# Expert-choice FFN: all block products of the hidden stage by inner products, gathers through the turned tokens' buffer, another order of sums in the output stages

## The chip, the cores and the metric

The kernel runs on one core of a Trainium2 chip. The metric is the device time of one execution in microseconds (us). The engines are named as in the profile: PE does matmuls, PEld loads their weights, DVE, ACT and POOL are the vector, scalar and GpSimd engines, and SP issues DMAs.

## The reference, cut to what matters

Eight sequences of 512 tokens of width D = 512 go through a modulated dense layer. A router gives each of E = 8 experts the k = 1024 tokens with the highest scores, each expert runs a two-layer network on its tokens, and the results are added back to the tokens' rows.

```python
y = ...                                  # modulated dense layer, (4096, 512)
scores = softmax(y @ Wr)                 # (4096, 8)
G, idx = top_k(scores.T, 1024)           # per expert
X_in = y[idx]                            # (8, 1024, 512)
h = gelu(einsum('ekd,edh->ekh', X_in, W1) + b1)      # hidden width 2048
X_e = einsum('ekh,ehd->ekd', h, W2) + b2
out = zeros.at[idx.reshape(-1)].add((G[..., None] * X_e).reshape(-1, 512))
return x + out.reshape(x.shape)
```

All of it is fp32.

## The kernel before

After a front (dense layer, router, choice of the tokens, some 165 us) the kernel works expert by expert (e = 0 to 7), each in two passes (p = 0, 1) over halves of the hidden width. A pass is a *hidden stage*, H = gelu(X W1 + b1), and an *output stage*, H W2, whose rows are scaled by the gain and added to DRAM by an indirect scatter. Both stages use the Strassen-Winograd scheme: a product of 2 x 2 blocks is made of seven block products and additions on DVE.

**Hidden stage.** There are seven outer products (numbered 1 to 7) of token sums with weight sums. Products 2 to 7 are themselves done by seven *inner products* of 128x256 outputs with K = 128 (`second_level`), in two halves a and b of the rows of the result. Product 1 is done *whole* (`one_product`): for each of four units two matmuls into a bank of 128x512 (`ps_a_h`), which ACT copies to `snap1` (L1215). The order of all steps on the engines follows a list written by hand, `ORDER`: "2b5" is inner product 5 of outer product 2, half b, "1.0" to "1.3" are the units of product 1, "h" stands for a leftover step of the output stage before. The first stage of all (e = p = 0) uses only the outer scheme (`hidden_unit`); the other fifteen follow ORDER.

An inner product's results are accumulated in PSUM banks. Tag a has two banks, tag b one, tag c two, and some of the a products lie in two banks of another pool. ACT evicts the a banks (L1129, L1153), DVE the b bank (L1138, inner product 2) and the c banks (L1149 after inner product 5, L1157 after inner product 4). When outer products are complete, DVE adds them (L1218, L1231, L1233, L1235) and ACT applies the gelu (L1219).

**Work between.** Behind certain steps of ORDER (the places of "1.0" to "1.3") other work is issued, ahead of the steps that follow it: at place 2 (behind "2b2 1.1") the four sums of W2's blocks on DVE (128x1024 each, L211 to L214), at place 0 of pass 1 the gathers of the next expert's tokens (`fetch`).

**Output stage.** Four units v, each of seven products of four matmuls 128x256 (`ps_a_o`, `ps_b_o`, `ps_c_o`), with four `left_sums` of H on DVE (128x512, L973 to L976), evictions by ACT and DVE (L1345 to L1391) and two scatters (L1378). `in_turns` interleaves the units. Between them lies other work: behind unit 2 the sums of the next pass's W1 (4 x 128x1024, then the second-level sums, 4 x 128x1024 for products 2, 7, 3, 4 in one tile `w1_l2` and 8 x 128x256 for products 5 and 6, L224 to L238), behind unit 0 of pass 1 `prepare(e+1)` (four transposes of the gathered tokens, L1018, four left sums of 128x1024, and their second-level sums, again 4 x 128x1024 and 8 x 128x256), behind unit 1 of pass 0 `indices(e+1)`.

**Tokens.** `gather` reads 128 rows at a time from DRAM by an indirect DMA on POOL's queue (L957) into tiles `row`, stores them to DRAM (`rows`, L961, SP's queue) and loads them turned into two tiles of tag `xg` (L963). The scatters of the output stage (L1378) are on POOL's queue too, and each adds to rows of one DRAM tensor.

Of the kernel before, what the change touches and what calls it, by code (L numbers as in the profile page):

```python
# [20 lines left out]
P = 128  # L21
# [4 lines left out]
def tile_modulated_expert_choice_ffn(  # L26
# [123 lines left out]
    for n in range(15):  # L150
# [18 lines left out]
    L2 = (2, 7, 3, 4)  # L169
# [3 lines left out]
        6a1 h 6a6 6a2 h 2a1 6a7 6a5 2a6 2a2 1.0 5a1 6a3 2a7 2a5 6a4 5a6 5a2 1.2 7a1  # L173
        2a3 5a7 5a5 2a4 7a6 7a2 4a1 5a3 7a7 7a5 5a4 4a6 4a2 3a1 7a3 4a7 4a5 7a4 3a6 3a2
        2b1 4a3 3a7 3a5 4a4 2b6 2b2 1.1 6b1 3a3 2b7 2b5 3a4 6b6 6b2 5b1 2b3 6b7 6b5 2b4
        5b6 5b2 1.3 7b1 6b3 5b7 5b5 6b4 7b6 7b2 3b1 5b3 7b7 7b5 5b4 3b6 3b2 4b1 7b3 3b7
        3b5 7b4 4b6 4b2 3b3 4b7 4b5 3b4 4b3 4b4
# [3 lines left out]
    def weight_blocks(kind, where, name):  # L181


        out = {}
        if kind == "w1":
            out["l2"] = wpool.tile([P, len(L2), 2, U * P], F32, tag="w1_l2", name=f"w1_l2_{name}")
        for (i, j), src in where.items():
            shape = [P, 2, U * P] if kind == "w1" else [P, U, QD]
            if kind == "w1" and (i, j) != (0, 0):
                t = out["l2"][:, L2.index({(1, 0): 2, (1, 1): 3, (0, 1): 7}[i, j]), :, :]  # L190
            else:
                t = wpool.tile(shape, F32, tag=f"{kind}_{i}{j}", name=f"{kind}_{i}{j}_{name}")
            if isinstance(src, list):
                for k in range(4):
                    nc.sync.dma_start(t[k * TB : (k + 1) * TB, :, :], src[k])
            else:
                nc.sync.dma_start(t, src)
            out[i, j] = t
        return out

    def weight_sum_steps(kind, blk, name):

        shape = [P, 2, U * P] if kind == "w1" else [P, U, QD]
        t1 = wpool.tile(shape, F32, tag=f"{kind}_t1", name=f"{kind}_t1_{name}")
        t2 = wpool.tile(shape, F32, tag=f"{kind}_t2", name=f"{kind}_t2_{name}")
        if kind == "w1":
            t4 = blk["l2"][:, L2.index(4), :, :]
        else:
            t4 = wpool.tile(shape, F32, tag=f"{kind}_t4", name=f"{kind}_t4_{name}")
# [6 lines left out]
    def weight_sums(kind, blk, name):  # L216
        for _ in weight_sum_steps(kind, blk, name):
            pass
        if kind == "w1":
# [11 lines left out]
            for which, base in ((5, blk["t1"]), (6, blk["t2"])):  # L231
                b = {(k, j): base[:, k, j * Q : (j + 1) * Q] for k in range(2) for j in range(2)}
                t = fx.tile([P, 3, Q], F32, tag=f"w1_sums{which}", name=f"w1_sums{which}_{name}")
                t1, t2, t4 = [t[:, n, :] for n in range(3)]
                nc.vector.tensor_add(t1, b[0, 0], b[0, 1])
                nc.vector.tensor_add(t2, t1, b[1, 1])
                nc.vector.tensor_add(t4, t2, b[1, 0])
                nc.vector.tensor_add(b[0, 1], b[0, 1], b[1, 1])  # L238
                blk["l2", which] = {**b, "t1": t1, "t2": t2, "t3": b[0, 1], "t4": t4}
# [636 lines left out]
    def indices(e):  # L876
# [4 lines left out]
        hot = rt2.tile([P, NT, KG], BF16, tag="hot", name=f"hot_{e}", bufs=1)  # L881
# [4 lines left out]
        val = rt2.tile([P, NT, 2, KG], BF16, tag="val", name=f"val_{e}", bufs=1)  # L886
# [57 lines left out]
    gathered = {}  # L944
# [3 lines left out]
    def gather(e, i):  # L948


        z = gp.tile([P, GH * YW], F32, tag="xg", name=f"xg_{e}_{i}")
        rows = dram.tile([HALF, YW], F32, name=f"rows_{e}_{i}")
        z = z[:, 0 : GH * D].rearrange("p (t c) -> p t c", c=P)
        for j in range(GH):
            g = i * GH + j
            to = gp.tile([P, YW], F32, tag="row", name=f"row_{e}_{g}")
            sent = nc.gpsimd.indirect_dma_start(  # L957
                out=to[:, :], out_offset=None, in_=y_dram[:, :],
                in_offset=bass.IndirectOffsetOnAxis(ap=idx[:, e, g : g + 1], axis=0),
            )  # L960
            nc.sync.dma_start(rows[j * P : (j + 1) * P, :], to)  # L961
        for q in range(4):
            nc.sync.dma_start(z[q * TB : (q + 1) * TB, :, :],  # L963
                              rows[:, q * P : (q + 1) * P].rearrange("(t a) c -> a t c", a=TB))
        with nc.allow_non_contiguous_dma(reason="512 values"):
            nc.sync.dma_start(gains[e][:, i * GH : (i + 1) * GH],
                              rows[:, D + e : D + e + 1].rearrange("(g p) o -> p (g o)", p=P))
        gathered[e, i] = z
        return sent

    def left_sums(a11, a12, a21, a22, s):
# [4 lines left out]
        nc.vector.scalar_tensor_tensor(s["s4"], s["s2"], -1.0, a12, op0=ALU.mult, op1=ALU.subtract)  # L976
# [3 lines left out]
    def token_tiles(e):  # L980
        l2 = fx.tile([P, len(L2), 2, HALF], F32, tag="x_l2", name=f"x_l2_{e}")
        base = {which: l2[:, m, :, :] for m, which in enumerate(L2)}
        xT = {(0, 1): base[2], (1, 1): base[4]}
        for k in range(2):
            xT[k, 0] = fx.tile([P, 2, HALF], F32, tag=f"xT{k}0", name=f"xT{k}0_{e}")
        s = {n: fx.tile([P, 2, HALF], F32, tag=f"x{n}", name=f"x{n}_{e}") for n in ("s1", "s2")}
        s["s3"], s["s4"] = base[7], base[3]
        gain = gains.pop(e)
        ngain = fx.tile([P, KG], F32, tag="ngain", name=f"ngain_{e}")
        tokens[e] = {**s, "11": xT[0, 0], "12": xT[0, 1], "22": xT[1, 1], "l2": l2}, gain, ngain  # L990
        return xT, s, gain, ngain

    def second_sums(e):
# [4 lines left out]
        more = fx.tile([P, 2, len(L2), Q], F32, tag="x_sums", name=f"x_sums_{e}")  # L998
        s2 = {"s1": a[1, 0], "s2": more[:, 0, :, :], "s3": more[:, 1, :, :],
              "s4": fx.tile([P, len(L2), Q], F32, tag="xT10", name=f"x_s4_{e}")}  # L1000
# [4 lines left out]
        for which, base in ((5, s["s1"]), (6, s["s2"])):  # L1005
            a = {(i, k): base[:, k, i * Q : (i + 1) * Q] for i in range(2) for k in range(2)}
            more = fx.tile([P, 3, Q], F32, tag=f"x_sums{which}", name=f"x_sums{which}_{e}")
            s2 = {"s1": a[1, 0], **{f"s{n + 2}": more[:, n, :] for n in range(3)}}
            left_sums(a[0, 0], a[0, 1], a[1, 0], a[1, 1], s2)
            s["l2", which] = {**s2, "11": a[0, 0], "12": a[0, 1], "22": a[1, 1]}  # L1010

    def prepare(e):
# [10 lines left out]
        second_sums(e)  # L1023

    def first_tokens(started):
# [4 lines left out]
        for j in range(GH):  # L1030
            for i in range(2):
                g = i * GH + j
                sent = nc.gpsimd.indirect_dma_start(
# [3 lines left out]
        with tc.issue_after(sent.ins):  # L1037
# [28 lines left out]
    def in_turns(units, between, keep=False):  # L1066
# [6 lines left out]
        for n in range(len(units)):  # L1073
# [12 lines left out]
            for work in between.get(n, ()):  # L1086
                with tc.issue_after(mark.ins):
                    work()
# [12 lines left out]
    def second_level(e, p, which, r, H, third):  # L1101
# [4 lines left out]
        if which in (5, 6):  # L1106
            lie = [sp.tile([P, HALF], F32, tag="snap4" if which == 5 else "snap2",
# [53 lines left out]
    def hidden_stage(e, p, H, between, held, then):  # L1161
# [3 lines left out]
        units = [one_product(e, p, u, H) for u in range(U)]  # L1165
        inner, left, mark = {}, {}, None
        place = [n for n, o in enumerate(ORDER) if "." in o and o[0] == "1"]
        place = {n: m for m, n in enumerate(place)}
        held = list(held)
        for n, o in enumerate(ORDER):  # L1170
            ready = []
# [4 lines left out]
            elif "." in o:  # L1176
                which, u = int(o[0]), int(o[2])
                units[u][which]()
                left[which, u] = True
                ready = [u]  # L1180
            else:
# [4 lines left out]
                todo = left.setdefault(("steps", which, r), set(range(1, 8)))  # L1186
                todo.discard(step)
                if not todo:
                    for u in (r, r + 2):
                        left[which, u] = True  # L1190
                        if which in (5, 6):
                            units[u][f"q{which}"](inner[which, r]["lie"][u // 2])
                    ready = [r, r + 2]
            for u in ready:
                units[u]["add"](left, u)
            if n in place:
                for work in between.get(place[n], ()):
                    with tc.issue_after(mark.ins):
                        work()

    def one_product(e, p, u, H):


        s, blk = tokens[e][0], w1_blocks[e, p]
        name = f"h{e}_{p}_{u}"
        bias = [b1_sb[:, e, p * HP + j * U + u : p * HP + j * U + u + 1] for j in range(2)]
        out = {(i, j): H[:, u, j, i * HALF : (i + 1) * HALF] for i in range(2) for j in range(2)}
        st, done = {}, set()

        def whole():  # L1210
            ps = bank("a", name, 2)
            product(ps, [blk[0, 0][:, k, u * P : (u + 1) * P] for k in range(2)],
                    [s["11"][:, k, :] for k in range(2)], True)
            st[1] = sp.tile([P, HALF], F32, tag="snap1", name=f"snap1_{name}", bufs=2)
            nc.scalar.copy(st[1], ps)  # L1215
# [5 lines left out]
        def add(there, u):  # L1221

            def can(name, *needs):
                if name in done or not all((n, u) in there or n in done for n in needs):
                    return False
                done.add(name)
# [268 lines left out]
```

## Time and profile before

| | us |
|---|---|
| median of 3 runs | 1692.82 (1692.28 to 1692.93) |
| the profiled execution, its own time | 1686.02 |
| its span in the profile | 1684.2 |
| hidden stage of expert 1, pass 1 | 465 to 506 |
| output stage after it | 506 to 558 |

The clock granted to PE is 0.996 of full speed in this execution. In a line of a timeline the columns are start, duration, engine, line of the kernel, operation, output and inputs, and in brackets how long the engine sat idle before it and what released it. Durations of neighbours overlap, so what one instruction costs in a row is read from the start to the next start. Inputs and outputs go by the program's names, with numbers left out: `ps_c_qc` is a c bank of a hidden stage, `ps_a_o` an a bank of an output stage, `w_t`, `w_sums`, `w_l` are sums and blocks of the weights, `hs_o` are left sums.

### The profile page before, as it was taken

How to read it: one execution, taken by the hardware profiler on the slowest of the kernel's cores; microseconds unless marked ns; L12 is line 12 of the kernel's file. 1: busy time of each engine (PE TensorE's matmuls, PEld its weight loads, DVE VectorE, ACT ScalarE, POOL GpSimd, SP SyncE). 2: the span in 40 equal slices, each digit the busy share in tenths (PEclk: the TensorE clock that was granted, in tenths of full speed). 3: DMA queues.
4: the chain of work that ended last, by engine and by line, in shares of the span. 5: the costliest groups of instructions: out<-in, count | busy, mean ns of one | idle time of the engine just before them, and what ended most of it. 6: DMA issues, size and time to landing. Idle time of an engine off the chain costs nothing.

```text
span 1684.2 us, 21423 instructions
## 1 busy us (share of the span) xinstructions
PE 1652.2 (98%) x7726; PEld 1335.6 (79%) x7726; DVE 1325.1 (79%) x2544; ACT 652.8 (39%) x1445; POOL 349.9 (21%) x238
## 2 busy tenths in 40 slices
PE   9997999999999999999999999999999999999997
PEld 5785567888878788888888788888888787888886
DVE  5885798978779686978789686978698786967681
ACT  3543323526152533425161524435261625344351
POOL 0111003220411213030412123030412132030202
PEclk9999999999999999999999999999999999999999
DMA  9724714742563337342653336342743247242403
GB/s 211 180 52 152 245 42 95 212 83 66 124 140 76 69 89 180 97 83 62 143 137 74 68 95 170 88 89 57 185 116 75 45 114 186 70 77 63 88 1 50
DMA packets 143273, 178.83 MB, mean 106 GB/s; under 512 B 16824, under 2 KB 92856, under 8 KB 143040
## 3 DMA queue, kind: packets, MB, share of 16 engines
q1 hardware_dynamic: 118240, 115.19, 24.2%
q0 software_dynamic: 24912, 62.27, 21.1%
q8 instruction: 60, 0.98, 0.3%
q14 instruction: 45, 0.37, 0.1%
q10 hardware_dynamic: 16, 0.02, 0.0%
HBM read 120.46 MB, written 65.37 MB: 110 GB/s over the span
## 4 chain that ended last, share of the span: by engine, by line
PE 71%; DVE 9%; DMA 1%; issue 1%; ACT 1%; POOLq 0%; POOL 0%; DVEq 0%
PE ps_a_o L1098 18%; PE ps_qa L1098 12%; PE ps_c_o L1098 10%; PE ps_c_qc L1098 9%; PE ps_a_qa L1098 6%; PE ps_a_h L1098 6%; PE ps_b_o L1098 5%; PE ps_b_qb L1098 5%; DMA out<-o_o,idx 1%; DVE x_l L1018 1%; DVE x_sums L975 1%; DVE x_sums L973 1%; DVE xs L974 1%; DVE hs_o L975 1%; DVE hs_o L973 1%
## 5 line engine op out<-in xcount | busy, mean ns | idle before, releaser
L1378 POOL DMA_INDIRECT out<-o_o,idx x128 | 257.2, 2009 | 1128.3 <-DVE o_o L1375 317.5
L1345 ACT ACTIVATE snap_o<-ps_a_o,gain 128x256 f32<-128x256 f32 x128 | 59.8, 472 | 332.2 <-PE ps_a_o L1098 315.0
L1129 ACT ACTIVATE q<-ps_qa 128x256 f32<-128x256 f32 x360 | 137.7, 383 | 127.7 <-PE ps_qa L1098 78.0
L1219 ACT ACTIVATE H<-H,b_sb 128x512 f32<-128x512 f32 x240 | 166.3, 718 | 37.3 <-DVE H L1218 31.9
L1098 PE MATMUL ps_a_o<-w,H 128*128 128x256 f32 x512 | 129.2, 383 | 3.4 <-ACT o_o L1386 3.4
L1098 PE MATMUL ps_b_o<-w,H 128*128 128x256 f32 x512 | 127.1, 379 | 0.0
L1098 PE MATMUL ps_a_o<-w_t,hs_o 128*128 128x256 f32 x512 | 123.8, 382 | 1.7 <-DVE hs_o L975 1.7
L1098 PE MATMUL ps_c_o<-w,hs_o 128*128 128x256 f32 x512 | 122.9, 382 | 0.0
L1098 PE MATMUL ps_c_o<-w_t,H 128*128 128x256 f32 x504 | 119.6, 380 | 2.8 <-DVE o_o L1370 2.8
L1098 PE MATMUL ps_a_o<-w,hs_o 128*128 128x256 f32 x512 | 121.8, 381 | 0.0
L1098 PE MATMUL ps_a_o<-w_t,H 128*128 128x256 f32 x512 | 121.3, 379 | 0.0
L1218 DVE TENSOR_TENSOR H<-H,q 128x512 f32<-128x512 f32 x180 | 118.3, 684 | 3.0 <-ACT H L1153 0.2
L1098 PE MATMUL ps_a_h<-xT,w 128*128 128x512 f32 x248 | 119.3, 593 | 0.0
L1098 PEld LDWEIGHTS ps_a_o<-w_t,hs_o 128*128 128x128 f32 x512 | 95.6, 190 | 20.4 <-DVE hs_o L975 4.1
L1098 PEld LDWEIGHTS ps_a_o<-w,H 128*128 128x128 f32 x512 | 95.5, 190 | 19.0 <-ACT o_o L1386 5.8
L1098 PEld LDWEIGHTS ps_c_o<-w,hs_o 128*128 128x128 f32 x512 | 95.9, 190 | 18.3 <-DVE hs_o L973 5.4
L1098 PEld LDWEIGHTS ps_c_o<-w_t,H 128*128 128x128 f32 x504 | 95.2, 190 | 16.9 <-DVE o_o L1370 4.0
L1098 PEld LDWEIGHTS ps_a_o<-w,hs_o 128*128 128x128 f32 x512 | 94.6, 190 | 16.8 <-ACT snap_o L1345 3.9
L1098 PEld LDWEIGHTS ps_b_o<-w,H 128*128 128x128 f32 x512 | 97.2, 190 | 13.5 <-DVE o_o L1356 0.3
L1098 PEld LDWEIGHTS ps_a_o<-w_t,H 128*128 128x128 f32 x512 | 96.3, 190 | 14.4 <-issue 0.5
L1345 ACT ACTIVATE snap_o<-ps_a_o,ngain 128x256 f32<-128x256 f32 x64 | 30.3, 473 | 175.0 <-PE ps_a_o L1098 175.0
L1129 ACT ACTIVATE q<-ps_a_qa 128x256 f32<-128x256 f32 x180 | 68.4, 380 | 59.0 <-PE ps_a_qa L1098 42.2
(357 smaller groups left out, 3338.9 us busy)
## 6 DMA issues: line engine op xcount, KB each, us to landing
w<-in_w SPq DMA_DIRECT2D x78, 512.0 KB, 5.0
w_l<-in_w SPq DMA_DIRECT2D x42, 512.0 KB, 5.0
rows<-row SPq DMA_DIRECT2D x56, 260.0 KB, 2.3
xg<-rows SPq DMA_DIRECT2D x56, 256.0 KB, 4.9
x<-in_x SPq DMA_DIRECT2D x28, 256.0 KB, 8.2
y_dram<-ytok SPq DMA_DIRECT2D x5, 1024.0 KB, 4.3
w_l<-in_w SPq DMA_DIRECT2D x24, 128.0 KB, 3.5
y_dram<-ytok POOLq DMA_DIRECT2D x12, 256.0 KB, 5.0
```

Source lines behind the costliest of these rows:

```text
L973: nc.vector.tensor_sub(s["s3"], a11, a21)
L974: nc.vector.tensor_sub(s["s1"], a22, a21)
L975: nc.vector.scalar_tensor_tensor(s["s2"], s["s3"], -1.0, a22, op0=ALU.mult, op1=ALU.subtract)
L1018: nc.vector.transpose(xT[i, k].rearrange("p j (t b) -> p t j b", b=TB), xg[:, :, 2 * k * TB : 2 * (k + 1) * TB].rearrange("p t (j a) -> p ...
L1098: nc.tensor.matmul(ps, lefts[k], rights[k], start=(start and k == 0), stop=(k == n - 1), skip_group_check=True)
L1129: nc.scalar.mul(t, st["a"], scale)
L1218: nc.vector.tensor_add(out[i, j], out[i, j], st[n])
L1219: nc.scalar.activation(out[i, j], out[i, j], AF.Gelu, bias=bias[j], scale=scale)
L1345: nc.scalar.mul(t, st["a"], scale)
L1378: nc.gpsimd.indirect_dma_start(out=last_rows[g] if e == E - 1 else out_rows, out_offset=bass.IndirectOffsetOnAxis(ap=idx[:, e, g : g + 1], ...
```

## The change

1. Outer product 1 is done by inner products too. The operands of all seven outer products lie in one tile (`w1_l2` and `x_l2`, seven slots), so that second-level sums become four instructions of 128x1792 each for the weights and four for the tokens. ORDER is rewritten: product 1 stands in it as "1a1" to "1b7", and "w" marks the four places for work between. The sums of W2 are issued at the third "w", behind 2b2.
2. `gather` puts the rows into four slots of the second `xg` tile, to which the second half's turned tokens go later. All eight gathers, stores and turned loads are issued behind the last scatter of the pass-0 output stage. Two small tiles of `indices` lie in the tail of the tile of b2.
3. In the output stages, the left sums of unit 1 are issued behind those of unit 0, and the work between is issued behind the latest left sums. `second_sums(e+1)` is no longer part of `prepare` at unit 0 and is issued at unit 1.
4. The turned tokens' block (1, 0) lies in the third part of the tile of the tokens' second-level sums.

The diff, cut to its core:

```diff
-    L2 = (2, 7, 3, 4)
+    L2 = (1, 2, 7, 3, 4, 5, 6)
     ORDER = """
-        6a1 h 6a6 6a2 h 2a1 6a7 6a5 2a6 2a2 1.0 5a1 6a3 2a7 2a5 6a4 5a6 5a2 1.2 7a1
-        2a3 5a7 5a5 2a4 7a6 7a2 4a1 5a3 7a7 7a5 5a4 4a6 4a2 3a1 7a3 4a7 4a5 7a4 3a6 3a2
-        2b1 4a3 3a7 3a5 4a4 2b6 2b2 1.1 6b1 3a3 2b7 2b5 3a4 6b6 6b2 5b1 2b3 6b7 6b5 2b4
-        5b6 5b2 1.3 7b1 6b3 5b7 5b5 6b4 7b6 7b2 3b1 5b3 7b7 7b5 5b4 3b6 3b2 4b1 7b3 3b7
-        3b5 7b4 4b6 4b2 3b3 4b7 4b5 3b4 4b3 4b4
+        1a1 h 1a6 2a1 1a2 h 1a7 1a5 2a6 2a2 w 6a1 1a3 2a7 2a5 1a4 6a6 6a2 5a1 2a3 6a7 6a5 2a4
+        5a6 5a2 w 7a1 6a3 5a7 5a5 6a4 7a6 7a2 4a1 5a3 7a7 7a5 5a4 4a6 4a2 3a1 7a3 4a7 4a5 7a4
+        3a6 3a2 2b1 4a3 3a7 3a5 4a4 2b6 2b2 w 1b1 3a3 2b7 2b5 3a4 1b6 1b2 6b1 2b3 1b7 1b5 2b4
+        6b6 6b2 w 5b1 1b3 6b7 6b5 1b4 5b6 5b2 7b1 6b3 5b7 5b5 6b4 7b6 7b2 3b1 5b3 7b7 7b5 5b4
+        3b6 3b2 4b1 7b3 3b7 3b5 7b4 4b6 4b2 3b3 4b7 4b5 3b4 4b3 4b4
     """.split()
...
-            for which, base in ((5, blk["t1"]), (6, blk["t2"])):
-                t = fx.tile([P, 3, Q], F32, tag=f"w1_sums{which}", name=f"w1_sums{which}_{name}")
-                nc.vector.tensor_add(t1, b[0, 0], b[0, 1])
-                nc.vector.tensor_add(t2, t1, b[1, 1])
-                nc.vector.tensor_add(t4, t2, b[1, 0])
-                nc.vector.tensor_add(b[0, 1], b[0, 1], b[1, 1])
...
-    def indices(e):
+    def indices(e, room):
...
-        hot = rt2.tile([P, NT, KG], BF16, tag="hot", name=f"hot_{e}", bufs=1)
+        hot = room[:, D : D + n].bitcast(BF16).rearrange("p (t k) -> p t k", k=KG)
...
-            to = gp.tile([P, YW], F32, tag="row", name=f"row_{e}_{g}")
+                to = zs[1][:, j * YW : (j + 1) * YW]
...
     def prepare(e):
...
         left_sums(xT[0, 0], xT[0, 1], xT[1, 0], xT[1, 1], s)
-        second_sums(e)
...
             for work in between.get(n, ()):
-                with tc.issue_after(mark.ins):
+                with tc.issue_after(behind.get("last", mark).ins):
                     work()
...
-        if which in (5, 6):
+        if which in (1, 5, 6):
...
-        def whole():
-            ps = bank("a", name, 2)
-            product(ps, [blk[0, 0][:, k, u * P : (u + 1) * P] for k in range(2)],
-                    [s["11"][:, k, :] for k in range(2)], True)
-            st[1] = sp.tile([P, HALF], F32, tag="snap1", name=f"snap1_{name}", bufs=2)
-            nc.scalar.copy(st[1], ps)
...
+        with tc.issue_after(summed["last"].ins) if v == 1 else ExitStack():
+            summed["last"] = left_sums(a[0, 0], a[0, 1], a[1, 0], a[1, 1], s)
...
     def fetch(e):
         gains[e] = fx.tile([P, KG], F32, tag="gain", name=f"gain_{e}", bufs=2)
-        for i in range(2):
-            gather(e, i)
+        with tc.issue_after(sent["last"].ins):
+            gather(e)
...
             if p == NP - 1 and e + 1 < E:
                 work[0] = [partial(prepare, e + 1)]
+                work[1] = [partial(second_sums, e + 1)]
```

## The prediction

> **What bounds the kernel now.** I read the page's engine shares first, then its groups, then the waits of PE, then one hidden stage and one output stage by windows and by timeline (expert 1, pass 1, which stands for the fifteen stages that follow ORDER).
>
> ```profile
> PE 1652.2 (98%) x7726; PEld 1335.6 (79%) x7726; DVE 1325.1 (79%) x2544; ACT 652.8 (39%) x1445; POOL 349.9 (21%) x238
> L1098 PE MATMUL ps_a_h<-xT,w 128*128 128x512 f32 x248 | 119.3, 593 | 0.0
> ```
>
> PE has almost no idle time, and DVE is next. The second line is product 1 of the hidden stages, whole.
>
> ```profile
> PE ps_a_o L1098 <- ACT o_o L1386: 3.4, 6, 0.6
> PE ps_c_o L1098 <- DVE o_o L1370: 2.8, 2, 1.5
> PE ps_a_o L1098 <- DVE hs_o L975: 1.7, 6, 0.3
> ```
>
> The waits of PE (total, times, longest): the first and third occur six times each, once in each pass-1 output stage of experts 1 to 6. The second falls at the ends of expert 0's two output stages.
>
> ```profile
> 465.00:484.70 19.70, 19.70 (x86) 15.80 (x85) 12.91 (x27) 11.09 (x28) 5.97 (x4) 1.00 0.61 129
> 484.70:506.00 21.30, 21.30 (x91) 16.78 (x90) 19.41 (x37) 13.88 (x33) 1.00 (x2) 1.00 0.57 134
> 506.00:558.00 52.00, 51.15 (x234) 43.52 (x233) 46.41 (x72) 11.91 (x25) 11.43 (x5) 1.00 0.38 91
> ```
>
> Windows, busy PE, PEld, DVE, ACT, POOL, then granted clock: first and second half of a hidden stage, then the output stage. DVE has 1.9 us to spare in the second half, and that half holds the four sums of w2:
>
> ```profile
> 485.62 0.41 DVE L1138 TENSOR_TENSOR H<-ps_b_qb,q 128x256 f32<-128x256 f32 x1
> 485.95 0.67 DVE L1218 TENSOR_TENSOR H<-H,q 128x512 f32<-128x512 f32 x1
> 486.55 1.21 DVE L211 TENSOR_TENSOR w_t<-w,w 128x1024 f32<-128x1024 f32 x1
> ...
> 490.07 1.22 DVE L213 TENSOR_TENSOR w_t<-w_t,w 128x1024 f32<-128x1024 f32 x1
> 491.21 0.41 DVE L1149 TENSOR_TENSOR H<-q,ps_c_qc 128x256 f32<-128x256 f32 x1
> 491.54 0.41 DVE L1157 TENSOR_TENSOR H<-ps_c_qc,q 128x256 f32<-128x256 f32 x1
> ```
>
> ```profile
> 484.69 0.59 PE L1098 MATMUL ps_b_qb<-x_l,w_l 128*128 128x256 f32 x2
> 485.13 1.88 PE L1098 MATMUL ps_a_h<-xT,w 128*128 128x512 f32 x4
> ...
> 490.73 1.02 PE L1098 MATMUL ps_a_h<-xT,w 128*128 128x512 f32 x2
> 491.67 0.70 PE L1098 MATMUL ps_c_qc<-x_l,w_sums 128*128 128x256 f32 x2
> ```
>
> DVE evicts no bank from 486.0 to 491.2. PE lives through it on whole products (128x512), which ACT evicts: 485.13 to 486.84 and 490.73 to 491.6. It still waits 0.07 at 491.67 for the eviction of 491.21.
>
> **Unit prices, from start-to-start times.** PE: a 128x256 product of two passes 0.432 us (488.14, 488.57, 489.00), a whole one 0.864 (two in 1.71). After a wait the second pass comes 0.10 later. DVE: 0.333 for 256 columns, 0.605 for 512, 1.14 for 1024; so 1792 columns are 1.14 + (1.14 - 0.333) = 1.95, an estimate by the straight line through 256 and 1024. From the end of a DVE eviction (0.41 after its start) to the PE start: 0.055.
>
> **1. Product 1 by inner products.** A hidden stage has 84 x 0.432 + 8 x 0.864 = 43.2 us of matmuls; after it has 98 x 0.432 = 42.3. Saved: 0.86 x 15 stages = -13.0. For DVE six evictions of 0.333 more per stage (+2.0); for ACT eight snaps of 0.38 instead of four copies of about 0.6, of an engine half idle in these windows. [...]
>
> **2. What lies behind the w2 sums.** They stay behind 2b2's eviction in ORDER, but the whole products around them are gone. Let PE start 2b2 at time 0 (484.69). DVE evicts it at 0.93, adds (0.605 after 0.333), then issues the sums, with 2b5's subtraction among them, then 3a4's eviction: start 0.93 + 0.333 + 0.605 + 4 x 1.14 + 0.333 = 6.76; end 7.17. On PE's list 1b7 takes that bank (c) and is 14th after 2b2: due 14 x 0.432 = 6.05, comes at 7.22. Stall 1.17 + 0.10. Next late: behind 3a4's eviction DVE has two output adds, then 1b2's eviction, which ends at 8.71; 6b2 needs that bank (b), second behind 1b7, comes at 8.76 instead of 7.22 + 0.54 + 0.43 = 8.19: 0.57 + 0.10. Then DVE and PE are level; margins behind it are 0.1 to 0.3. Sum 1.95 a stage. Before, the same place costs 0.07 + 0.11 and 0.04 + 0.11 (starts 491.67 and 493.54) = 0.32. So +1.63 x 15 = **+24.5**. Bounds: if the second stall vanishes +0.95 each (+14); if it passes on into the thin margins twice more by some 0.3, +2.2 each (+33). The 1.73 us of whole products removed from behind 2b2, added to the 0.32, give 2.05, so I keep 1.95. First half: no place found late; it has 27 DVE instructions of 12.9 us in 19.7.
>
> **3. Sums.** w1's second sums become four of 1.95 (7.8) for 4 x 1.14 + 8 x 0.333 = 7.2, likewise those of the tokens. Both lie in output stages, DVE 46.4 of 52: +1.1 makes 47.5 of 50.6. Cost 0 while that slack of 3 covers it; without it, up to +1.1 x 7. [...]
>
> **4. Order in the output stages.** The token sums (prepare with second_sums, about 16 us of DVE: four transposes and four left sums of 1.14, and 7.2) lie in unit 0, and left sums of unit 1 come late behind them:
>
> ```profile
> 529.38 1.89 PE L1098 MATMUL ps_a_o<-w,hs_o 128*128 128x256 f32 x8
> 531.84 1.99 PE L1098 MATMUL ps_a_o<-w,H 128*128 128x256 f32 x8 [0.56 <-ACT o_o L1386]
> 534.12 1.13 PE L1098 MATMUL ps_a_o<-w_t,hs_o 128*128 128x256 f32 x4 [0.29 <-DVE hs_o L975]
> ```
>
> 531.84 is 0.73 behind 529.38 + 8 x 0.216, and 534.12 0.45 behind; with 0.10 each for second passes 1.38. With second_sums in unit 1, behind its last left sum, I find no bank late: -1.38 x 6 = **-8.3**. Bounds: nothing saved (the 7.8 us stall unit 1 as much) to -8.3.
>
> **5. Gathers.** Issued behind the last scatter of the pass-0 output stage, no longer between scatters: at the end of expert 0's pass 1 the wait for a scatter (1.5 in the row, 1.75 by starts with the second pass) and a 0.2 before it go, **-1.9** (bounds -2 and 0). The other wait of that row, at 274 in pass 0, is the scatters' own chain and stays. On POOL's queue eight gathers now stand behind the eight scatters. On SP's queue the eight row stores, eight turned loads and two gains move behind the w2 loads, the next w1 loads stay behind them. Rows of the chain from the last scatter to the first transpose (gathers issue 1.3 us apart and land after 4.3):
>
> ```profile
> 481.54 1.86 POOL L1378 DMA_INDIRECT out<-o_o,idx  x1 [4.04 <-DVE q L1235]
> rows<-row SPq DMA_DIRECT2D x56, 260.0 KB, 2.3
> xg<-rows SPq DMA_DIRECT2D x56, 256.0 KB, 4.9
> 514.91 1.24 DVE L1018 STREAM_TRANSPOSE xT<-xg 128x1024 f32<-128x1024 f32 x1
> ```
>
> First gather issued at 483.7, landed 488.0, its store 490.3 frees its slot; the second four issue until 495.5, land 499.8, are stored 502.1; the last turned load lands at 507. The first transpose starts at 514.9, so the rest of the hidden stage hides it with some 7 us to spare. Cost 0; beyond the margin each us costs 1 us in seven stages.
>
> **6. Expert 0, pass 1.** indices(1) (5.4 us of DVE) shares that hidden stage and loses the whole products as cover: +1 (0 to 2). The front, the first tokens and the layout issue the same instructions: 0 +/- 2.
>
> **Sum.** -13.0 + 24.5 - 8.3 - 1.9 + 1 = +2.3. The profiled execution took 1686.0 (span 1684.2 and 1.8 around it), which makes 1688.3; the median of the runs shown is 6.8 above that execution, so 1692.8 + 2.3 = **1695**.
>
> **The rivals.**
> *Short stall.* DVE gets through the sums in time, only 0.32 to 0.65 per stage is lost, as before or twice that (3a4's eviction goes in between the sums): -13.0 + 0 to 5 - 8.3 - 1.9 = 1670 to 1675. For it: 2b5's subtraction already goes in between; against: the before shows no eviction from 486.55 to 491.21.
> *Late tokens (slower).* One of the two DMA rounds through four slots waits longer, since w2 loads compete; the turned tokens come after 514.9. Decides from 7 us on; 2 us beyond it cost 7 x 2 = 14: 1709. For it: the hidden stage's DMA share is 0.6 here and turned loads wait for stores. Against: the margin.
> *Longer stalls (slower).* The margins of 0.1 to 0.3 behind 6b2 fail and the loss is the upper bound of part 2, 0.57 a stage more than taken: 1695 + 0.57 x 15 = 1703.
> *No effect.* The saving on PE is taken back by DVE, prepare's wait only moves to unit 1, and the two terms cancel within 3 us: 1692.
>
> **How the numbers follow.** Forecast 0.45 (own range 1688 to 1701: 0.07 faster, 0.19 within, 0.19 slower), short stall 0.20, late tokens 0.12, longer stalls 0.18, no effect 0.05. This kernel's measurement can tell 0.2% (3.4 us) from no change. Faster 0.07 + 0.20, same 0.19 + 0.05, slower 0.19 + 0.12 + 0.18. The range reaches part of the way to either rival: 1680 to 1708 leaves out the lowest tenth and the worst of late tokens.
>
> **What would show it.** Right: PE work of a hidden stage 42.3; two PE waits per hidden stage behind 2b2, of about 1.2 and 0.6, released by DVE evictions; the two output rows of six gone; L1018 not waiting for a DMA. Wrong: no such waits in hidden stages (short stall), transposes that wait for turned loads (late tokens), or waits in output unit 1 or 2 behind instructions of 1792 columns.

## The result, and the profile after

The changed kernel takes 1708.32 us (median of 4 runs, 1707.09 to 1711.59) against 1692.78 beside it: ratio 1.0095, 95% interval 1.0083 to 1.0106, about 15.5 us slower. The profiled execution took 1707.1, span 1705.3; that of before had a span of 1684.2. The two traces thus differ by 21.1, more than the medians do; why is part of the answer below.

The engines' line of the page after, and the windows of expert 1, pass 1 (two halves of the hidden stage, then the output stage; busy PE, PEld, DVE, ACT, POOL, clock, DMA):

```profile
PE 1644.4 (96%) x7906; PEld 1372.6 (80%) x7906; DVE 1370.8 (80%) x2450; ACT 667.7 (39%) x1505; POOL 338.2 (20%) x238
```

```profile
480.13:501.00 20.87, 20.87 (x98) 18.39 (x97) 15.95 (x34) 12.76 (x32) 8.15 (x7) 1.00 0.59 136
501.00:523.50 22.50, 21.12 (x98) 17.69 (x96) 20.36 (x39) 14.02 (x34) 4.13 (x4) 1.00 0.90 204
523.50:573.00 49.50, 49.50 (x229) 42.96 (x228) 46.13 (x53) 11.13 (x24) 11.43 (x6) 1.00 0.47 113
```

PE is busy for 7.8 us less than before, in a span 21 longer. In these windows it is idle only in the second half of the hidden stage (21.12 of 22.50); the output stage, which had 0.85 idle, has none.

The waits of PE in the changed kernel (what waited, for what, total, times, longest):

```profile
PE ps_c_qc L1081 <- DVE H L1140: 14.7, 15, 1.1
PE ps_style L81 <- DMA cond_sb<-in_condT: 9.7, 1, 9.7
PE ps_b_qb L1081 <- DVE q L1121: 6.1, 15, 0.4
...
PE ps_a_h_a L81 <- DVE x_l L1036: 3.3, 1, 3.3
PE ps_c_o L1081 <- DVE o_o L1336: 2.8, 1, 2.8
```

The rows of before for the left sums and for ACT's `o_o` (six times each) are gone. In their place stand two rows of fifteen, one wait of each kind in each hidden stage, and three single waits: one at the very start, one among the first tokens, one near 1321 us.

The stage of expert 1, pass 1, by timeline, PE first and then DVE:

```profile
505.16 0.59 PE L1081 MATMUL ps_a_qa<-x_l,w_l 128*128 128x256 f32 x2
506.73 0.70 PE L1081 MATMUL ps_c_qc<-x_sums,w_l 128*128 128x256 f32 x2 [0.97 <-DVE H L1140]
507.26 0.59 PE L1081 MATMUL ps_a_qa<-x_l,w_sums 128*128 128x256 f32 x2
508.26 0.70 PE L1081 MATMUL ps_b_qb<-x_l,w_l 128*128 128x256 f32 x2 [0.41 <-DVE q L1121]
```

```profile
500.44 0.41 DVE L1121 TENSOR_TENSOR H<-ps_b_qb,q 128x256 f32<-128x256 f32 x1
500.77 0.68 DVE L1179 TENSOR_TENSOR H<-H,q 128x512 f32<-128x512 f32 x1
501.37 1.22 DVE L208 TENSOR_TENSOR w_t<-w,w 128x1024 f32<-128x1024 f32 x1
502.51 0.42 DVE L1132 TENSOR_TENSOR H<-q,ps_c_qc 128x256 f32<-128x256 f32 x1
502.85 1.22 DVE L209 TENSOR_TENSOR w_t<-w_t,w 128x1024 f32<-128x1024 f32 x1
...
506.26 0.42 DVE L1140 TENSOR_TENSOR H<-ps_c_qc,q 128x256 f32<-128x256 f32 x1
506.59 1.28 DVE L1179 TENSOR_TENSOR H<-H,q 128x512 f32<-128x512 f32 x2
507.79 0.42 DVE L1121 TENSOR_TENSOR q<-ps_b_qb,q 128x256 f32<-128x256 f32 x1
```

This is the place of the prediction's part 2: 506.73 is 1b7, which waits for 3a4's eviction of 506.26, and 508.26 is 6b2, which waits for 1b2's of 507.79. By starts the two waits are 1.13 and 0.57, and 0.10 each for the second pass: 1.91 a stage, where 1.95 was forecast.

From start to start, a pass 0 (hidden and output stage) of experts 1 to 6 takes 93.15 us before and 93.91 after (+0.76). A pass 1 takes about 93.6 before and 92.91 after (-0.68). The two nearly cancel. The trace's 21.1 us lie elsewhere:

| | before, us | after, us | difference added |
|---|---|---|---|
| first router product starts | 34.56 | 46.35 | +11.8 |
| last matmul of the first product of output stage (0, 0) | 223.53 | 240.15 | +4.8 |
| hidden stage of (1, 0) starts | 371.28 | 386.22 | -1.7 |
| from there to the end of the last product | 1303.89 | 1309.95 | +6.1; the output stage of (5, 1) takes 4.6 more than the other pass-1 output stages |

### The profile page after: what moved, and what is told of

Same layout as the page of the kernel before. It is cut to its first block, busy times and chain, and to the rows that moved or that the text cites. A ratio compares the mean times of both kernels' runs of the same rounds, so it can differ in the third digit from the quotient of the medians.

```text
span 1705.3 us, 21772 instructions
## 1 busy us (share of the span) xinstructions
PE 1644.4 (96%) x7906; PEld 1372.6 (80%) x7906; DVE 1370.8 (80%) x2450; ACT 667.7 (39%) x1505; POOL 338.2 (20%) x238
## 5 line engine op out<-in xcount | busy, mean ns | idle before, releaser
L1344 POOL DMA_INDIRECT out<-o_o,idx x128 | 247.2, 1931 | 1157.3 <-DVE o_o L1341 384.6
L1112 ACT ACTIVATE q<-ps_qa 128x256 f32<-128x256 f32 x450 | 168.6, 382 | 144.9 <-PE ps_qa L1081 100.4
L1179 DVE TENSOR_TENSOR H<-H,q 128x512 f32<-128x512 f32 x240 | 159.7, 686 | 22.7 <-ACT H L1136 12.3
L1081 PE MATMUL ps_c_qc<-x_sums,w_l 128*128 128x256 f32 x420 | 126.6, 383 | 14.7 <-DVE H L1140 14.7
L1081 PE MATMUL ps_b_qb<-x_l,w_l 128*128 128x256 f32 x420 | 126.6, 383 | 6.1 <-DVE q L1121 6.1
L1081 PE MATMUL ps_c_qc<-x_l,w_sums 128*128 128x256 f32 x420 | 125.0, 379 | 0.0
L1081 PEld LDWEIGHTS ps_a_o<-w,hs_o 128*128 128x128 f32 x512 | 95.1, 190 | 15.7 <-ACT snap_o L1311 2.4
```

The source lines that it names most:

```text
L1081: nc.tensor.matmul(ps, lefts[k], rights[k], start=(start and k == 0), stop=(k == n - 1), skip_group_check=True)
L1112: nc.scalar.mul(t, st["a"], scale)
L1179: nc.vector.tensor_add(out[i, j], out[i, j], st[n])
L1344: sent["last"] = nc.gpsimd.indirect_dma_start(out=last_rows[g] if e == E - 1 else out_rows, out_offset=bass.IndirectOffsetOnAxis(ap=idx[:, ...
```

## The experiments

**The changed kernel again, and the load of the condition vector.** The single waits were not in the forecast. e1_again is the changed kernel once more.

> The changed kernel once more, to see what in its trace recurs. Theory: the wait of the style product for the condition vector (9.7 us in the trace) and the two waits of each hidden stage behind 2b2 (1.135 and 0.567, with 0.10 each for the second pass) recur to the last digit, since they come from the order of instructions; the 3.3 us wait among the first tokens at 185 and the 2.8 us wait at 1321 behind a scatter that took 11 us are of this one execution and are gone or elsewhere. Time about 1708. Rival: all of them recur, then the late scatter and the first tokens are made by the change too.

Measured: 1706.4 (ratio 1.0091, 1.0075 to 1.0106). The waits behind 2b2 recur (14.8 and 6.1 in all) and so does the first wait (8.6). But the wait among the first tokens recurs too (3.5) and so does the one near expert 5's end (3.0): the rival was right that these two are not single accidents. Whether the change makes them is for the runs below.

The order of SP's queue explains the first. These are the DMA issues of before, then of the changed kernel:

```profile
0.75 0.43 SPq L360 DMA_DIRECT2D aff_sb<-in_affT  x1
1.24 0.46 SPq L362 DMA_DIRECT2D cond_sb<-in_condT  x1
1.74 0.97 SPq L408 DMA_DIRECT2D x<-in_x  x2
```

```profile
1.24 0.97 SPq L396 DMA_DIRECT2D x<-in_x  x2
2.25 1.95 SPq L402 DMA_DIRECT2D wa_sb<-in_weightT  x4
...
7.31 0.39 SPq L350 DMA_DIRECT2D cond_sb<-in_condT  x1
```

The lines that load the condition vector are the same in both kernels. Their place in memory is not. The change moves two tiles of 1536 bytes per partition (`hot` and `val`) out of a pool that lies below the front's tiles; everything above slides down, and in the program as built `cond_sb` goes from address 81792 to 80256, into the region of a set-up pool that ends at 81408. Its load now waits for a POOL instruction that fills a tile of that pool (before, it waits for nothing), and the scheduler issues it behind the weights and the first part of the second sequence. On PE the style product then starts at 14.27 instead of 4.96. The clock granted to PE is 0.75 up to 15 us and 0.88 from 15 to 40, where before has 1.00 in both; that fits a first router product that is 11.8 late after a wait of 9.7.

```diff
+    with tc.tile_pool(name="room", bufs=1) as below, \
             tc.tile_pool(name="p1c", bufs=1) as p1c, ...
+        below.tile([P, 3 * P], F32, name="below")
```

> The changed kernel with 1536 unused bytes per partition below the front's tiles, so that the condition vector's tile lies at the address that it has in the kernel before, above the tiles of the set-up pool. Theory: the load of the condition vector waited for the set-up pool whose place it took, and stood behind the weights on SP's queue; with the room it is second on the queue again, the 9.7 us wait is gone, and the start of the first router product goes from 46.35 back to 34.6: -11.8, 1696.5. Rival: the wait is the DMA engines' load in that execution, or is hidden later behind the routing; then the time stays at 1708.

Measured: 1695.4 (ratio 1.0023, 1.0014 to 1.0033), 11.0 below e1_again. The load is second on the queue again, and the wait is gone. The first router product starts at 36.77, not at 34.6; e5_before_trace below, with the order of before, has it at 36.01. e6_before_late makes the reverse test on the kernel before.

```diff
-        nc.sync.dma_start(cond_sb, condT.rearrange("(k p) b -> p k b", p=P))
...
         load_x(1)
+        nc.sync.dma_start(cond_sb, condT.rearrange("(k p) b -> p k b", p=P))
```

> The kernel before with one line moved: the load of the condition vector is issued behind the weights and the second sequence, where it stands on SP's queue in the changed kernel, and nothing else. Theory: the front costs as much as in the changed kernel, 8.6 to 9.7 us of wait and some of a cold clock: 1691.4 + 11 = 1702, give or take 2. Rival: part of it is hidden behind loads that the front waits for anyway: under 1696.

Measured: 1701.13 against 1691.57 (ratio 1.0052, 1.0037 to 1.0067; 9.6 us). One line in its later place costs the kernel before as much. Here PE waits 13.5 us for the vector, since its load stands still later on the queue (10.90 us instead of 7.31).

**The hold among the first tokens.** e5_before_trace is the kernel before once more.

> The kernel before, once more, for a second trace of it. The profiled execution of before took 1686.0, its other executions about 1691.4 to 1692.8; the traces of all five variants of the changed kernel have a hold of PE of some 3.5 us and a slower clock behind it (5 us together) at the second transposes of the first tokens, and before's one trace has not. Theory: the hold is not made by the change; before has it in most executions, and the 5 to 7 us between its trace and its other executions are this hold: this trace shows it, span about 1690. Rival: the hold is made by the change: this trace is without it, span about 1684, or it is longer for another reason.

Measured: span 1690.4. Its waits of PE now have this row:

```profile
PE ps_a_h_a L81 <- DVE xT L1053: 3.2, 1, 3.2
```

So the hold is no work of the change; the one profiled execution of before was without it. It accounts for the +4.8 of the table. That is what most of the 6.8 us between that execution and the median were, which the prediction carried along as a constant. With e5's trace the difference to the changed kernel is 14.9, in line with the medians.

**The waits behind 2b2.** In e4_spread the sums of W2 are taken apart.

```diff
-        5a6 5a2 w 7a1 ... 7a6 7a2 4a1 ... 4a6 4a2 3a1 ... 3a6 3a2 2b1 ... 2b6 2b2 w 1b1 ... 6b6 6b2 w 5b1
+        5a6 5a2 7a1 ... 7a6 7a2 w 4a1 ... 4a6 4a2 w 3a1 ... 3a6 3a2 w 2b1 ... 2b6 2b2 w 1b1 ... 6b6 6b2 5b1
...
+                        steps[key] = weight_sum_steps("w2", w2_blocks[key], f"{key[0]}_{key[1]}")
+                    next(steps[key])
+                work = {n: [step] for n in range(1, 5)}
```

> As e2_front, with the four sums of W2 no longer in one piece behind 2b2 but one each behind 7a2, 4a2, 3a2 and 2b2. Theory: the stall behind 2b2 is DVE's 4.9 us without a bank eviction; single sums of 1.14 us fit the margins, so both waits go: 1.91 x 15 = -28.6, 1668. Rival: DVE has no room anyway (its work of a hidden stage is 35.5 of 42.3 us) and the wait only moves to other places: within 8 us of e2_front, over 1688.

Measured: 1684.84 (ratio 0.9964, 0.9951 to 0.9978), 10.6 below e2_front. Both rows of waits are gone, but a pass-0 hidden stage falls from 43.37 to 42.52 only, since waits of 0.05 to 0.25 with their second passes add up to 1.06 a stage. Neither number of the expectation was met. e8_halves cuts each sum into two of 128x512, at eight places:

```diff
+            for h in (slice(0, U // 2), slice(U // 2, U)):
+                yield nc.vector.tensor_add(to[:, h, :], a[:, h, :], b[:, h, :])
...
+                work = {n: [step] for n in range(1, 9)}
```

> As e4_spread, with each sum of W2 cut into two of 128x512, at eight places from 5a2 to 1b5. In e4_spread there remain waits of 1.0 us per hidden stage (second passes included) behind the single sums of 1.14 us. Theory: what counts is how long DVE goes without an eviction; pieces of 0.605 fit: up to -1.0 x 15 = -15 against e4_spread, 1670 to 1680. Rival: what is left has to do with DVE's whole work in the second half, or eight pieces cost more start-up: within 3 us of e4_spread.

Measured: 1672.71 (ratio 0.9881, 0.9867 to 0.9896), within the range expected. A hidden stage takes 41.75. DVE's work is the same as in e2_front but for a few starts, PE's too; spreading the sums is worth 0.85 us a stage (e4_spread), halving the pieces at twice as many places another 0.77, together 1.62. The page of e8_halves:

```profile
PE 1640.6 (98%) x7906; PEld 1375.7 (82%) x7906; DVE 1370.7 (82%) x2510; ACT 659.4 (39%) x1505; POOL 348.2 (21%) x238
```

DVE's busy time is 1370.6 in e2_front and 1370.7 here: the engine was not short of time, it was late at the wrong moments.

**The order of the sums in the output stages.** e3_second_back undoes part of it on the changed side, e7_before_sums does it alone on the side of before.

```diff
 e3:            work[0] = [partial(prepare, e + 1), partial(second_sums, e + 1)]
 e7: (before)   left sums of unit 1 behind those of unit 0, work between behind left sums,
                work[0] = [partial(prepare, e + 1)]; work[1] = [partial(second_sums, e + 1)]
```

> As e2_front, with the tokens' second-level sums issued again right behind prepare in unit 0 of the output stage, 4 x 128x1792. Theory: the left sums of unit 1 (now ahead of the work between) no longer come late, or, if they do, the 1.38 us stall of each pass-1 output stage of experts 1 to 6 comes back: between 1696.5 and 1705. Rival: with 7.8 us of sums in one piece behind 9.2 us of prepare, evictions of unit 1 wait much longer, 3 us or more per stage: over 1715.

Measured: 1701.9 (ratio 1.0065, 1.0052 to 1.0079), 6.5 above e2_front. In its trace each of the seven pass-1 output stages of experts 0 to 6 takes 50.8 to 51.4 instead of 49.54 (1.3 to 1.8), and most of that is waits for `o_o` (6.6 us in 7 waits). The time is in the range expected, but what came back is not the wait for left sums.

> The kernel before with part 3 of the change alone: left sums of unit 1 behind those of unit 0, the work between behind the latest left sums, second_sums at unit 1 (with its 4 x 128x1024 and 8 x 128x256). Theory: the stall of 1.38 us in six output stages goes and nothing comes in its place: -8.3, 1683. Rival: in before, the small sums leave evictions of unit 1 late: -4 or less.

Measured: 1686.14 (ratio 0.9966, 0.9953 to 0.9979): -5.4, between the expectation and its rival. The waits for left sums are gone. Where nothing comes in between, a pass-1 output stage falls from 50.57 to 49.11 (-1.46). In three of the six it takes 50.7 to 52.1, and PE waits for `o_o` instead:

```profile
PE ps_c_o L1098 <- DVE o_o L1373: 6.3, 4, 1.7
```

```profile
547.87 8.55 POOL L1381 DMA_INDIRECT out<-o_o,idx  x1 [3.99 <-DVE w_l L214]
```

The second fence is POOL's timeline of the same kernel: a scatter whose issue takes 8.55 us, where three quarters of the changed kernel's take 1.54 to 1.99; the other two stages have one of 8.82 and one of 10.44. `o_o` has two buffers, and the next unit cannot write one before its scatter has read it.

**Long issues of scatters.** In the changed kernel an issue takes over 5 us once, in expert 5, pass 1. POOL's line, DVE's timeline and the window of it:

```profile
1292.54 10.97 POOL L1344 DMA_INDIRECT out<-o_o,idx  x1 [6.62 <-DVE o_o L1336]
```

```profile
1292.44 2.02 DVE L963 TENSOR_TENSOR x_sums<-x_l 128x1792 f32<-128x1792 f32 x1
1294.38 0.68 DVE L963 TENSOR_TENSOR hs_o<-H 128x512 f32<-128x512 f32 x1
...
1299.45 2.02 DVE L966 SCALAR_TENSOR_TENSOR x_sums<-x_sums,x_l 128x1792 f32<-128x1792 f32 x1
1301.38 0.68 DVE L965 SCALAR_TENSOR_TENSOR hs_o<-hs_o,H 128x512 f32<-128x512 f32 x1
1301.99 0.48 DVE L1322 SCALAR_TENSOR_TENSOR o_o<-ps_b_o,gain,snap_o 128x256 f32<-128x256 f32 x1
```

```profile
1292.00:1304.00 12.00, 12.00 (x57) 10.58 (x56) 12.00 (x13) 1.90 (x4) 10.97 (x1) 1.00 0.00 0
```

The last two columns are the DMA share and GB/s: nothing moves for twelve microseconds. DVE runs sums of two SBUF tensors back to back, and the scatter's issue ends at 1303.51, 1.52 behind the first DVE instruction that reads a PSUM bank (1301.99). A scatter whose issue is not held up takes 1.54 (the shortest of the 128). In e7_before_sums the issue of 547.87 ends 1.50 behind the PSUM input at 554.92. Of the ten scatters of the changed kernel whose issue takes 3 us or more, seven end 1.49 to 1.52 behind such an input. The other three end 1.49 to 1.51 behind the start of a sum of two SBUF inputs (L224; at 565.23 for the scatter of 563.70), so it is not always a PSUM input that stands 1.5 us ahead of such an end; the reason stays open.

Why this scatter and not its likes? In the other six pass-1 output stages of experts 0 to 6 the same scatter starts 0.03 ahead of the first sum of 1792 columns and takes 1.56 or 1.57. In expert 4, POOL and then DVE:

```profile
1105.39 1.56 POOL L1344 DMA_INDIRECT out<-o_o,idx  x1 [6.50 <-DVE o_o L1357]
```

```profile
1105.42 2.03 DVE L963 TENSOR_TENSOR x_sums<-x_l 128x1792 f32<-128x1792 f32 x1
```

In expert 5 its release comes one DVE instruction later (L1336 in the brackets, not L1357), it starts 0.10 behind that sum, and its issue lasts through the run, 10.97. A shift of 0.12 us goes with the 4.6.

A sum of two SBUF inputs does not hold up every issue: the six scatters of 1.56 or 1.57 are issued while the first sum of 1792 columns runs. By what means a run of them lengthens an issue no trace shows; measured are the ends.

e12_split tests the length of the run: the tokens' second-level sums in two parts, on e8_halves.

```diff
-                work[1] = [partial(second_sums, e + 1)]
+                work[1] = [partial(second_sums, e + 1, 0)]
+                work[2] = [partial(second_sums, e + 1, 1)] + work[2]
```

> As e8_halves, with the four second-level sums of the tokens in two parts: two at unit 1, two at unit 2 ahead of the sums of W1. In every trace of the changed order the 145th indirect DMA (expert 5, pass 1) takes 10.97 us on POOL, in a window in which the DMA engines are idle and DVE runs sums of two SBUF inputs back to back (1292.4 to 1302.0 in the changed kernel's trace); it ends 1.5 us behind the first DVE instruction with a PSUM input (1301.99), as the long issues of e7_before_sums and before do. Theory: POOL cannot write the scatter's descriptors while DVE runs instructions that read two SBUF tensors; with half the run between evictions the issue at that place is under 7 us, PE's wait of 2.7 there is gone or under 1, -3 to -5 against e8_halves by ratio 0.985 to 0.987; the place may move to unit 2, where the run of sums is now longer. Rival: the long issue is a matter of the 145th DMA alone (a ring, a counter): 10.97 again, ratio as e8_halves, 0.988.

Measured: 1667.46 against 1693.15 (ratio 0.9854, 0.9838 to 0.9871). POOL's and DVE's timeline at the same scatter:

```profile
1262.48 7.09 POOL L1363 DMA_INDIRECT out<-o_o,idx  x1 [6.62 <-DVE o_o L1355]
```

```profile
1262.39 2.01 DVE L1004 TENSOR_TENSOR x_sums<-x_l 128x1792 f32<-128x1792 f32 x1
...
1267.46 0.68 DVE L977 SCALAR_TENSOR_TENSOR hs_o<-hs_o,H 128x512 f32<-128x512 f32 x1
1268.07 0.48 DVE L1341 SCALAR_TENSOR_TENSOR o_o<-ps_b_o,gain,snap_o 128x256 f32<-128x256 f32 x1
```

It ends at 1269.57, again 1.50 behind the PSUM input. The issue was a shade over the 7 us expected, and of PE's wait of 2.7 there 0.3 is left; the output stage is 4.0 shorter than in e8_halves. From the start of the first sum to the PSUM input it is 5.68 instead of 9.55 in the changed kernel, and the issue is 3.88 shorter: the length follows the run of sums, not the count of DMAs. What the expectation says of POOL was the author's theory; no trace shows what POOL does in these times. The ratio is the lowest of the study.

**Gathers, product 1, idle matmuls.** e10_gather lets the gathers go as soon as their indices are there:

```diff
-        with tc.issue_after(sent["last"].ins):
-            gather(e)
+        gather(e)
```

> As e8_halves, with the gathers no longer held back behind the last scatter of the pass-0 output stage; they go on POOL's queue as soon as their indices are there, between the scatters, as in the kernel before. Theory (part 2 of the change as the prediction costed it): the wait for a scatter at the end of expert 0's pass 1 comes back, +1.9, and the rest stays hidden: 1674 to 1675. Rival A: scatters behind gathers come late in every expert (as in e7_before_sums, where their issue took 5 to 9 us in several stages and PE waited): +4 to +10. Rival B: nothing, 1672.7.

Measured: ratio 0.9886 (0.9871 to 0.9901), as e8_halves: neither the 1.9 nor 4 to 10. Its hidden and output stages take the same times as in e8_halves but for that of the late scatter (2.0 longer). The gathers of experts 2 to 7 do go early (expert 2's from 432.79 on, between scatters), and the stages show no cost of it. At the end of expert 0's pass 1 no wait comes back, but there the run tests nothing: expert 1's gathers stand behind the eight scatters in this kernel too, and in the kernel before (last scatter 291.10, first gather 293.05). The wait at 369.45 there has another source, a scatter with a long issue that ends 1.49 behind a PSUM input; POOL, then DVE:

```profile
359.99 4.90 POOL L1378 DMA_INDIRECT out<-o_o,idx  x1 [3.97 <-DMA out<-o_o,idx]
```

```profile
363.40 0.47 DVE L1356 SCALAR_TENSOR_TENSOR o_o<-ps_b_o,gain,snap_o 128x256 f32<-128x256 f32 x1
```

e11_before_both is e7_before_sums with W2's sums in eight pieces, by the same `step`, at eight places of its own ORDER; product 1 stays whole.

```diff
+            elif o == "w":
+                with tc.issue_after(mark.ins):
+                    between["w"][0]()
```

> As e7_before_sums (the kernel before with part 3 alone), with the sums of W2 in eight pieces over its own ORDER; product 1 stays whole and the gathers stay as before. What remains between it and e8_halves is part 1 without its stall, and part 2. Theory: the 0.32 us of waits per hidden stage go, -4.8 against e7_before_sums: 1681; and e8_halves lies below it by the saving on PE, 13, less what scatters add there: 8 to 13. Rival: the saving on PE is not worth 0.86 per stage: a difference under 5.

Measured: 1682.83 against 1687.97 (ratio 0.9974, 0.9965 to 0.9983), no better than e7_before_sums by ratio. An undisturbed hidden stage takes 42.69 instead of 43.00 (-0.31, as expected), but four pass-1 hidden stages take 43.8 to 44.5, with waits for c banks of up to 1.4, and the scatters still cost two output stages. The difference to e8_halves, by ratio 0.0093 or 15.7 us, is more than the 8 to 13 expected; the disturbed stages are part of it. An undisturbed pass is 0.52 longer than in e8_halves in both kinds (92.80 and 92.28 for pass 0), where the saving on PE was reckoned at 0.86. The remaining 0.3 lies in e8_halves: at two places of each of its hidden stages a product still comes 0.05 late and its second pass 0.10 later (572.76 and 581.98 in expert 2's pass 0), and e11_before_both has nothing of the kind there.

```profile
572.28 0.59 PE L1093 MATMUL ps_c_qc<-x_sums,w_l 128*128 128x256 f32 x2
572.76 0.70 PE L1093 MATMUL ps_qa<-x_l,w_sums 128*128 128x256 f32 x2
573.29 0.59 PE L1093 MATMUL ps_c_qc<-x_l,w_sums 128*128 128x256 f32 x2
```

So the products themselves save 0.52 + 0.31 = 0.83 a pass.

The last run is about the hold among the first tokens, on e8_halves:

```diff
-        idle(IDLE2, ps_mm.tile([P, HALF], F32, tag="b", name="ps_idle2"))
+        for _ in range(4 * IDLE2):
+            in_order(partial(nc.tensor.matmul, ps_idle[:, 0:P], ones, ones, start=True, stop=True))
```

> As e8_halves, with the 16 idle matmuls of 512 columns ahead of the first tokens as 64 of 128 columns, the same time on PE but 96 more instructions. The hold of PE at the second transposes of the first tokens comes after the same count of PE's instructions in every trace (1974 records), and ends about 1 to 2 us behind a 16 KB transfer of the instruction queue; such a transfer comes every 256 or so of PE's records. Theory: PE waits for its own code there. With 96 more instructions ahead the point lies among the idle matmuls, which wait for the gathers anyway: the hold of 3.4 and the slow clock behind it go, -3 to -5 against e8_halves: 1668 to 1670. Rival: the hold comes from the gathers or the transposes: it stays where it is, 1672.7.

Measured: ratio 0.9885 (0.987 to 0.99). The trace has no hold; but e10 and e11, which ran beside it, have none either, without extra instructions, and the kernel before takes 1687.97 there, some 3.5 less than beside e1 to e8. These three ran on another chip than the runs ahead of them. So this run decides nothing about the hold, and that PE waits for its code there was not shown.

## Why the prediction was right or wrong

It said 1695, range 1680 to 1708, with 0.49 for slower. The sign was the likelier one, and the time lies just above the range; but most of the 15.5 us come from a term that stood at nothing.

The step that failed is in part 6: "The front, the first tokens and the layout issue the same instructions: 0 +/- 2." The front has the same lines, but not the same order: the load of the condition vector went from second to after the weights on SP's queue. That costs 11.0 (e1_again to e2_front) or 9.6 (e6_before_late). Layout was read as a matter of space; it is also one of dependencies. Without that the changed kernel takes 1695.4. That this is the 1695 of the forecast is in part luck: the kernel before takes 1691.38 beside it, so the difference is 4.0 where 2.3 was forecast, and the terms below miss in both directions.

Going by the other terms:

- Part 1, -13.0: the count of matmuls stands. e11_before_both against e8_halves shows 0.52 a pass, and 0.83 without the two small waits that are left there, of the 0.86 forecast.
- Part 2, +24.5 for the stall: 1.91 a stage instead of 1.95, at the two places named, released by the two evictions named. Taking the block of sums apart (e8_halves) gives 1.62 a stage back.
- Parts 1 and 2 together: forecast +0.77 a stage, +0.76 in a pass 0.
- Part 4, -8.3: right in sign. A pass 1 gains 1.44 beyond the hidden stage's +0.76 (0.68 + 0.76; forecast 1.38). But "I find no bank late" left out POOL: the sums in their new place hold up one scatter in expert 5, and 4.6 us are lost there. e7_before_sums shows it three times.
- Part 5, -1.9: the wait is gone, and so is its 1.75, but the reason given is wrong. Expert 1's gathers never stood between these scatters. In the kernel before, a scatter's long issue (4.90 at 359.99) frees `o_o` late, and PE waits for it. e7_before_sums, with the gathers as before and the sums in another order, loses that wait: from the first inner product to the start of the next hidden stage 4.78 (370.97 to 375.75) instead of 6.54 (364.74 to 371.28). So it belongs to part 4. The other wait of that row, 1.3 at 274, which was to stay, is missing in the changed kernel's trace and 1.0 in e1_again's. That the table's -1.7 is near -1.9 is chance: it also holds the loss of that second wait and a longer hidden stage.
- Part 6, +1 for indices(1): about +0.7. The hidden stage of (0, 1) takes 1.24 longer than that of (1, 0) before (44.24 and 43.00) and 1.96 longer after (45.33 and 43.37).
- The rivals: late tokens did not happen; no transpose waits for a turned load. Short stall did not happen by itself; e8_halves, with the sums cut, comes near its time.

The prediction also measured its sum against a profiled execution that lacked a hold of about 5 us which the others have. A difference of 6.8 between profile and median was a sign to ask what that execution lacked.

## What to carry to other kernels

A change that moves tiles between pools also moves addresses, and a tile that slides onto a closed pool's region can delay a load at the very start (here from 1.24 to 7.31 us, which cost 11.0): compare the order of each queue from its first line, also where the source is unchanged. An engine with time to spare on average (DVE was busy for 80% of the span) can still stall its neighbour when a block of long instructions stands between two evictions (PE lost 1.91 us a stage); cutting the same work into pieces of 0.6 us and spreading them gave 1.62 us in each of fifteen stages at no cost in DVE's busy time (1370.6 and 1370.7). Where POOL issues indirect DMAs, look for long runs of DVE sums of two SBUF inputs beside them, and let an eviction from PSUM fall in between, or let the scatter start ahead of the run: here an issue took 10.97 us beside such a run, 7.09 with the eviction earlier, and 1.56 or 1.57 where it started 0.03 ahead.

## What was not expected of the hardware

The hold of PE among the first tokens lasts 3.2 to 3.5 us and falls at the same tile (`ps_a_h_a`, L81) in every trace that has it; in the changed kernel it is 3.26, after 974 matmuls. Behind it the granted clock is lower (0.52 from 185.0 to 188.4 in the changed kernel), and the same work takes about 5 us more in all (180.52 to 188.45, against 168.82 to 171.83 in the trace of before that has no hold). A transfer of 16 KB on the instruction queue comes, in the changed kernel, every 256 of PE's records (matmuls and weight loads) on average, 182 to 331 apart. One falls within the hold (183.43 to 184.33) and ends 0.7 us ahead of PE's next matmul. The trace of before without the hold has such a transfer too, from 171.64 to 172.60, 1.7 us behind the start of the matmul that the hold would have delayed (169.94). What makes the difference was not settled.
